# A mixture's first choice of experts is made in the attention layer in front of it

## The chip, the cores and the metric

The kernel runs as one program on one core of one Trainium2 chip. Its time is the device time of that core in microseconds, from one execution to the next; a profile of one execution shows every instruction on TensorE (PE, with its weight loads as PEld), VectorE (DVE), ScalarE (ACT), GpSimd (POOL) and the DMA queues (SyncE's among them, SP).

## What is computed

Eight layers are applied to x of 4 sequences, 1024 positions and 128 features, each as `x = x + layer(layernorm(x))`: a causal attention of 16 heads (AttentionA), a mixture of 8 experts, a gated attention, the same mixture again, a state space layer, a gated feed-forward layer, a second causal attention and the feed-forward layer again. The change bears on the two mixtures and the two layers in front of them. The mixture, cut to what matters:

```python
capacity = int(T / E * CAP_FACTOR)
probs = jax.nn.softmax(x @ Wr, axis=-1)
topk_probs, topk_experts = jax.lax.top_k(probs, K)
e_flat = topk_experts.reshape(B, S)
onehot = jax.nn.one_hot(e_flat, E, dtype=jnp.int32)
pos_all = jnp.cumsum(onehot, axis=1) - onehot
pos = jnp.take_along_axis(pos_all, e_flat[..., None], axis=-1)[..., 0]
keep = pos < capacity
buf = buf.at[e_flat, b_idx, pos_c].add(x_rep * keep[..., None])
h = jax.nn.relu(jnp.einsum('ebnc,ech->ebnh', buf, W1) + b1[:, None, None, :])
y = jnp.einsum('ebnh,ehc->ebnc', h, W2) + b2[:, None, None, :]
out = (y[e_flat, b_idx, pos_c] * keep * p_flat).reshape(B, T, K, C).sum(axis=2)
```

Every position picks its two likeliest experts (K = 2 of E = 8); each expert has 160 places per sequence, given out in the order of the positions, and what finds no place is dropped.

## The kernel before

x of all sequences stays in SBUF as eight chunks of 128 positions by 128 features per sequence (`k.xb(b)`). The layers follow one another in the list LAYERS; a layer opens its pools of SBUF and PSUM tiles when it begins and closes them at its end, and the pools of the next layer lie at the same addresses. Some layers (Begun) begin inside the layer in front of them: a Start object calls their first steps, with PSUM banks (`start.bank`) and an order (`start.pin`) lent by that layer. GatedAttention is begun inside the first mixture so. The mixture itself isn't: it begins when its layer is called.

A framework orders the instructions of each engine ahead of time, by their dependencies and their place in the program, and puts the semaphores in; an engine then works through its queue in order. Where the program wants an order of its own, it pins it: `k.order()` gives a function that chains instructions one behind the other on their engine. In all layers around the change the instructions on PE are pinned in the order of the program.

The mixture, Mixture.__call__, works through four sequences. For each, `normalized(b)` makes the normalised x, xl (L117 to L131: bn_stats, bn_aggr, Sqrt on ACT, reciprocal, eight TENSOR_SCALAR). `route(b)` is the choice, a generator that gives way at several points: eight transposes of xl into xt (L600, copied out of PSUM by DVE or ACT in turn, L108 and L110), the logits lg (L605), softmax over 8 experts (L617 to L624), the two best with ties broken by a rank table (L629 to L640), `taken` (L646); then the count of those before a position, cnt (L654), run and pos (L661, L662), spot (L665, L666), and rows and share for the later gather (L671 to L679). `dispatch(b)` builds for each chunk a 0/1 matrix d by comparing spot with the iota `place` (L691) and multiplies xl with it into the PSUM tiles acc (L696), which are copied to buf (L704). `experts(b)` runs the two matrices of every expert and calls the next sequence's route between them. So the choices of sequences 1 to 3 lie inside the experts of the sequence before, while that of sequence 0 stands at the head of the layer, before anything else of it:

```python
normalized(0)
for _ in route(0):
    pass
```

AttentionA works on 32 pairs of heads (n, eight per sequence), four groups gq of query blocks each. Small jobs wait in the list `pieces` and are called by `outputs(n, gq)`: one at the head of each of its steps (GROUPS gives 1, 1, 2 and 2 steps to the four groups), and a second one in a step when more than three wait. In a step the transposes of the probabilities p (L482) come first on PE, then the products of the step before with v (L497, into o), then scores further ahead (L374). Jobs are the projections, the product with Wo of a finished pair (L340, added to sum_t on DVE, L344), and after a sequence's last pair the transposes of sum_t (L350) and the addition to x (L352). All jobs share one PSUM bank, tag m, with a single buffer.

GatedAttention's `attend(b, other, before)` runs 16 steps for a sequence: a score product (L1012), bias on DVE (L1015), Relu and Square on ACT (L1018, L1019), and the product with v (L997) of the score of two steps before. In each step it also calls one step of `before` (output of the sequence before: L1037, L1042) and one of `other` (preparation of the next sequence). For the last sequence `other` is empty. Its bank for such steps, tag pt, has two buffers. After the steps the result is multiplied with ut (L1006) and then by the output weights (L1037).

Of the kernel before, what the change touches and what calls it, by code (L numbers as in the profile page):

```python
# [20 lines left out]
P = 128  # L21
B = 4
T = 1024
C = 128
NC = T // P
# [4 lines left out]
NEXP = 8  # L30
TOPK = 2
FF = 512
CAP = int(T / NEXP * 1.25)
# [143 lines left out]
class Start:  # L177

    def __init__(self, k, layer):
        self.k, self.open = k, True
        self.gen = layer.run(self)
        next(self.gen)

# [16 lines left out]
class AttentionA:  # L202
# [34 lines left out]
        )  # L237
        self.bo = k.broadcast_row(w, "bo", C, nc.sync)

    def __call__(self, start=None):  # L240
        k, tc, nc = self.k, self.k.tc, self.k.nc
        wq, wk, wv, wo, bo = self.wq, self.wk, self.wv, self.wo, self.bo
        Q, NQ, NP = self.Q, self.NQ, HEADS // 2
        scale = 1.0 / math.sqrt(DH_A)
        with self.stack as ctx:
# [14 lines left out]
            pieces = []  # L260
# [248 lines left out]
            for n in range(B * NP):  # L509
                for gq in range(NQ):  # L510
                    if gq == 1 and n + 3 < B * NP and (n + 3) % NP == 0:
                        normal = normalized((n + 3) // NP)
                    if 0 < gq < 3:
                        next(normal, None)
                    if gq == 0 and n + 2 < B * NP and (n + 2) % NP == 0:
                        across((n + 2) // NP)
                    if gq == 1 and n > 0:
                        joined(n - 1)
                    if gq == 3 and n + 2 < B * NP:
                        projected(n + 2)  # L520
                    outputs(n, gq)
            behind.pop(0)()
            joined(B * NP - 1)
            while pieces:
                pieces.pop(0)[1]()

# [4 lines left out]
class Mixture:  # L531
# [7 lines left out]
    def __init__(self, k: Kernel):  # L539
# [22 lines left out]
        self.ones = w.tile([P, P], F32, name="ones")  # L562
        nc.gpsimd.memset(self.ones, 1.0)

    def __call__(self, start=None):
        k, tc, nc, ex = self.k, self.k.tc, self.k.nc, self
        rows, share = self.rows, self.share
# [3 lines left out]
        with ExitStack() as ctx:  # L571
# [16 lines left out]
            def normalized(b):  # L588
                xls[b] = sb.tile([P, NC, C], F32, tag="xl", name="xl")
                k.normalize(xls[b], k.xb(b))  # L590

            def route(b):


                xl = xls[b]
                xt = sb.tile([P, T], F32, tag="xt", name="xt")
                for h in range(2):
                    ps = ps_t.tile([P, 512], F32, tag="pt", name="ps")
                    for c in range(4):
                        pe(nc.tensor.transpose(ps[:, c * P : (c + 1) * P], xl[:, h * 4 + c, :], k.ident))  # L600
                    k.evacuate(xt[:, h * 512 : (h + 1) * 512], ps)
                    yield
                lg = ps_l.tile([P, NC, NEXP], F32, tag="lg", name="lg")
                for c in range(NC):
                    pe(nc.tensor.matmul(  # L605
                        lg[:, c, :], xt[:, c * P : (c + 1) * P], ex.wr, start=True, stop=True
                    ))
                shape = [P, NC, NEXP]

                def wide(t):  # L610
                    return t.unsqueeze(2).to_broadcast(shape)

                def column(tag):
                    return k.small.tile([P, NC], F32, tag=tag, name=tag)

                top = column("top8")
                nc.vector.tensor_reduce(top, lg, AX.X, ALU.max)  # L617
                pr = sb.tile(shape, F32, tag="pr", name="pr")
                nc.vector.tensor_tensor(pr, lg, wide(top), ALU.subtract)
                nc.scalar.activation(pr, pr, AF.Exp)  # L620
                total = column("total")
                nc.vector.tensor_reduce(total, pr, AX.X, ALU.add)
                nc.vector.reciprocal(total, total)
                nc.vector.tensor_tensor(pr, pr, wide(total), ALU.mult)  # L624

                hot, prob, first = [], [], []
                for n in range(TOPK):
                    best = column(f"best{n}")
                    nc.vector.tensor_reduce(best, pr, AX.X, ALU.max)  # L629
                    h = sb.tile(shape, F32, tag=f"hot{n}", name="hot")  # L630
                    nc.vector.tensor_tensor(h, pr, wide(best), ALU.is_equal)

                    nc.vector.tensor_tensor(h, h, ex.rank.unsqueeze(1).to_broadcast(shape), ALU.mult)
                    r = column(f"rank{n}")
                    nc.vector.tensor_reduce(r, h, AX.X, ALU.max)
                    nc.vector.tensor_tensor(
                        h, wide(r), ex.rank.unsqueeze(1).to_broadcast(shape), ALU.is_equal
                    )
                    if n + 1 < TOPK:
                        nc.vector.scalar_tensor_tensor(pr, h, -2.0, pr, ALU.mult, ALU.add)  # L640
                    hot.append(h)
                    prob.append(best)
                    first.append(r)

                taken = sb.tile(shape, F32, tag="taken", name="taken")
                nc.vector.tensor_tensor(taken, hot[0], hot[1], ALU.add)  # L646
                yield
                yield
                yield

                cnt = ps_l.tile([P, 2, NC, NEXP], F32, tag="lg", name="cnt")
                flat = taken.rearrange("p c e -> p (c e)")
                for n, table in enumerate((ex.before, ex.ones)):
                    pe(nc.tensor.matmul(  # L654
                        cnt[:, n, :, :].rearrange("p c e -> p (c e)"), table, flat, start=True, stop=True
                    ))
                pos = sb.tile(shape, F32, tag="pos", name="pos")
                run = sb.tile(shape, F32, tag="run", name="run")
                nc.vector.memset(run[:, 0, :], 0.0)
                for c in range(1, NC):  # L660
                    nc.vector.tensor_tensor(run[:, c, :], cnt[:, 1, c - 1, :], run[:, c - 1, :], ALU.add)  # L661
                nc.vector.tensor_tensor(pos, cnt[:, 0, :, :], run, ALU.add)  # L662

                spot = sb.tile(shape, F32, tag="spot", name="spot")
                nc.vector.scalar_tensor_tensor(spot, pos, 1.0, taken, ALU.add, ALU.mult)  # L665
                nc.vector.tensor_scalar(spot, spot, -1.0, None, ALU.add)  # L666
                spots[b] = spot

                for n in range(TOPK):
                    mine = sb.tile(shape, F32, tag="mine", name="mine")  # L670
                    nc.vector.tensor_tensor(mine, hot[n], pos, ALU.mult)  # L671
                    at = column(f"at{n}")
                    nc.vector.tensor_reduce(at, mine, AX.X, ALU.add)
                    kept = column(f"kept{n}")
                    nc.vector.tensor_scalar(kept, at, float(CAP), None, ALU.is_lt)
                    nc.vector.tensor_tensor(share[:, b, :, n], kept, prob[n], ALU.mult)

                    nc.vector.tensor_scalar(at, at, float(CAP - 1), float(SLOTS), ALU.min, ALU.add)
                    nc.vector.scalar_tensor_tensor(  # L679
                        rows[:, b, :, n], first[n], -float(CAP), at, ALU.mult, ALU.add  # L680
                    )

            def dispatch(b, between):

# [114 lines left out]
                    if i + GOT < len(pairs):  # L799
                        fetch(i + GOT)  # L800

            normalized(0)
            for _ in route(0):
                pass
            left, behind = [], iter(())

            def close():
# [27 lines left out]
class GatedAttention(Begun):  # L835
# [37 lines left out]
    def run(self, start):  # L873
# [6 lines left out]
        with ExitStack() as ctx:  # L880
# [878 lines left out]
@with_exitstack  # L1759
def kernel(ctx: ExitStack, tc: tile.TileContext, ins: dict, out: bass.AP):  # L1760
    k = Kernel(ctx, tc, ins, out)
    made = {layer: layer(k) for layer in LOADS if layer in LAYERS}
    begun = None
    for n, layer in enumerate(LAYERS):
        layer = made[layer]
        if isinstance(layer, Begun):
            if begun is None:
                begun = Start(k, layer)
            begun.finish()
            begun = None  # L1770
# [113 lines left out]
```

## Time and profile before

| | us |
|---|---|
| three timed runs | 3298.49, 3306.97, 3306.78 |
| their median | 3306.78 |
| the profiled execution | 3300.56 |
| its span, first to last instruction | 3298.8 |
| AttentionA's last o product ends | 1152.74 |
| first mixture's first choice, from xl to spot | 1159.38 to 1174.94 |
| GatedAttention's last sequence, steps | 1557 to 1597 |
| second mixture's first choice, from xl to spot | 1602.78 to 1619.38 |
| instructions in all | 46096 |

The times in the lower rows are counted from the start of the span of the profiled execution. Busy times are sums over all layers, and the limits differ from layer to layer, so the part of the trace around a layer's border says more about this change than the totals. In lines of the order of time, the first number is the start, the second the length, then come engine, line, operation, the tile written, the tiles read and the shapes; "x8" stands for eight instructions drawn together, and the bracket gives the idle time before them with what ended it. Fp32 products appear twice per call.

### The profile page before, as it was taken

Reading aid. Unit: us, or ns where it says so; the run is one execution under the profiler, and the core shown is the slowest. Engines: PE = TensorE matmul, PEld = TensorE weight load, DVE = VectorE, ACT = ScalarE, POOL = GpSimd, SP = SyncE. Lnnn points to the kernel's source line nnn. Section 1 sums busy time; section 2 is a strip of 40 time slices with the busy share of each in tenths; the row PEclk is TensorE's granted clock in tenths of the full one; section 3 lists DMA queues with packets and bytes.
Section 4 is the critical chain, followed back from the end, with each engine's and each line's share of the span. In section 5 each row is a group of like instructions: output and inputs, shape, how many; then the busy total and the mean of one; then the engine's idle time right before and its main releaser. Section 6 shows DMA issues by size and latency. Waiting matters only on the chain. (4 is left out here: it accounts for less than half of the span.)

```text
span 3298.8 us, 46096 instructions
## 1 busy us (share of the span) xinstructions
PE 2965.1 (90%) x16624; PEld 1696.0 (51%) x16624; DVE 2324.5 (70%) x5415; ACT 1819.5 (55%) x3822; POOL 285.0 (9%) x297
## 2 busy tenths in 40 slices
PE   7999999999999988699898588888778899999988
PEld 4555555555555556445566244454445444444435
DVE  5777777778777666676564788888977767676634
ACT  4555555556555523355333797988643365556662
POOL 3000000000000013510034000000002101010000
PEclk9999999999999989899999799999998799899999
DMA  3110000000000001100011111111102111111100
GB/s 109 44 33 17 14 18 17 14 18 17 14 17 17 16 13 35 61 0 0 0 35 42 59 57 53 56 55 54 66 22 62 30 37 50 31 50 31 31 2 26
DMA packets 84901, 109.39 MB, mean 33 GB/s; under 512 B 26048, under 2 KB 66544, under 8 KB 82240
## 3 DMA queue, kind: packets, MB, share of 16 engines
q1 hardware_dynamic: 59136, 69.50, 6.6%
q0 software_dynamic: 18688, 30.65, 3.5%
q10 hardware_dynamic: 6848, 6.29, 0.6%
q8 instruction: 130, 2.13, 0.3%
q14 instruction: 99, 0.81, 0.1%
HBM read 90.76 MB, written 15.60 MB: 32 GB/s over the span
## 5 line engine op out<-in xcount | busy, mean ns | idle before, releaser
L389 ACT ACTIVATE p<-p,tops 128x640 f32<-128x640 f32 (+7 forms) x512 | 392.2, 768 | 287.6 <-DVE tops L387 226.3
L380 DVE CUSTOM_DVE_ANT_0 p<-s,mask 128x512 f32<-128x512 f32 (+3 forms) x768 | 392.1, 551 | 130.3 <-PE s L374 129.8
L1635 ACT ACTIVATE p<-x 128x512 f32<-128x512 f32 (+3 forms) x768 | 337.6, 490 | 246.3 <-PE x L1634 176.5
L1574 DVE TENSOR_REDUCE tops<-s 128x2 f32<-128x1024 f32 (+3 forms) x384 | 361.2, 955 | 133.5 <-PE s L1570 94.0
L1277 PE MATMUL acc<-hc,ident 128*128 128x512 f32 x512 | 269.7, 650 | 93.2 <-ACT hc L1276 92.4
L374 PE MATMUL s<-kt,qt 64*128 64x512 f32 (+3 forms) x1536 | 311.3, 516 | 20.2 <-DVE tops L380 19.8
L482 PEld LDWEIGHTS t<-ident,p 128*128 128x128 f32 x2304 | 263.0, 141 | 80.8 <-issue 66.7
L1264 DVE TENSOR_TENSOR_SCAN st<-decay,st 128x1024 f32<-128x1024 f32 x128 | 288.7, 2278 | 10.8 <-ACT decay L1261 10.3
L497 PE MATMUL o<-pt,vv 128*64 128x256 f32 (+1 forms) x2560 | 291.2, 365 | 0.0
L482 PE MATMUL t<-ident,p 128*128 128x128 f32 x2304 | 283.7, 273 | 1.6 <-ACT p L389 1.6
L1629 PE MATMUL x<-q,k 75*128 75x512 bf16 (+3 forms) x768 | 222.6, 337 | 27.8 <-ACT p L1635 15.0
L488 ACT COPY pt<-t 128x512 f32<-128x512 f32 (+1 forms) x320 | 155.0, 495 | 156.9 <-DVE pt L490 148.8
L1565 PE MATMUL s<-k,q 72*128 72x512 bf16 (+3 forms) x768 | 217.7, 350 | 24.4 <-DVE tops L1574 17.1
L1276 ACT ACTIVATE hc<-ps,by_time 128x256 f32<-128x256 f32 x512 | 200.3, 477 | 49.6 <-PE ps L1270 49.5
L490 DVE COPY pt<-t 128x512 f32<-128x512 f32 x320 | 212.2, 684 | 16.5 <-PE t L482 16.3
L497 PEld LDWEIGHTS o<-pt,vv 128*64 128x64 f32 x2560 | 166.8, 136 | 96.7 <-issue 28.6
L374 PEld LDWEIGHTS s<-kt,qt 64*128 64x128 f32 x1536 | 124.5, 187 | 146.0 <-issue 77.9
L1277 PEld LDWEIGHTS acc<-hc,ident 128*128 128x128 f32 x512 | 91.6, 198 | 208.9 <-ACT hc L1276 190.5
L1263 DVE TENSOR_TENSOR st<-du,bs 128x1024 f32<-128x1024 f32 x128 | 151.8, 1216 | 48.5 <-PE ps L1270 48.3
L696 PE MATMUL acc<-d,xl 128*128 128x480 f32 (+1 forms) x384 | 154.2, 563 | 28.0 <-DVE d L691 28.0
L1270 PEld LDWEIGHTS ps<-ident,st 128*128 128x128 f32 x1024 | 126.2, 147 | 96.3 <-issue 60.5
L1663 PE MATMUL o<-p,vx 128*32 128x512 f32 (+3 forms) x1536 | 171.8, 519 | 0.0
(302 smaller groups left out, 4763.8 us busy)
## 6 DMA issues: line engine op xcount, KB each, us to landing
bs<-b_rows SPq DMA_DIRECT2D x64, 512.0 KB
share<-shares SPq DMA_DIRECT2D x256, 64.0 KB
k<-b_parts POOLq DMA_DIRECT2D x16, 576.0 KB, 12.5
q<-b_parts POOLq DMA_DIRECT2D x48, 192.0 KB, 11.6
shares<-rows SPq DMA_DIRECT2D x512, 0.5 KB
b_parts<-part SPq DMA_DIRECT2D x24, 256.0 KB
w_W<-in_W_dram ACTq DMA_DIRECT2D x16, 256.0 KB
y_rows<-y SPq DMA_DIRECT2D x16, 192.0 KB
```

The source lines that it names most:

```text
L374: pe(nc.tensor.matmul(s[:, h, : hi - lo], q[feats, ib * P : (ib + 1) * P], kk[feats, lo:hi], start=True, stop=True,))
L380: ve(nc.vector.tensor_tensor_reduce(p[:, h, i, lo:hi], s[:, h, : hi - lo], m, -1.0, 3.4e38, ALU.add, ALU.min, tops[:, h, i, at : at + 1],))
L389: exp = nc.scalar.activation(p[:, h, i, :width], p[:, h, i, :width], AF.Exp, bias=tops[:, h, i, 0:1], scale=-1.0, accum_out=sums[:, h, i : ...
L482: pe(nc.tensor.transpose(t[:, m, h, i * P : (i + 1) * P], p[:, h, i, jb * P : (jb + 1) * P], k.ident))
L490: nc.vector.tensor_copy(pt[:, :, lo:], t[:, m, :, lo:])
L497: pe(nc.tensor.matmul(o[feats, lo:], pairs[n]["v"][:, jb, feats], pt[:, h, lo:], start=jb == 0, stop=jb == (gq + 1) * Q - 1,))
L1264: nc.vector.tensor_tensor_scan(st, decay, st, 0.0, ALU.mult, ALU.add)
L1277: nc.tensor.matmul(acc[:, c : c + 2, :].rearrange("p c d -> p (c d)"), k.ident, hc.rearrange("p c d -> p (c d)"), start=n == 0, stop=n == ...
L1565: start.pin(nc.tensor.matmul(s[:, a, : hi - lo], qq[:ROWS, two + a, ib * P : (ib + 1) * P], kk[:ROWS, two + a, lo:hi], start=True, stop=ha ...
L1574: nc.vector.tensor_reduce(tops[:, half, two : two + 2, n], s[:, :, : hi - lo], AX.X, ALU.max)
L1629: start.pin(nc.tensor.matmul(x[:, lo:], kk[:FULL, a, jb * P : (jb + 1) * P], qq[:FULL, a, hq * 512 + lo : (hq + 1) * 512], start=True, sto ...
L1635: nc.scalar.activation(p[:, a, lo:], x[:, lo:], AF.Exp)
```

## The change

The choice of sequence 0 becomes a method, `choice`, with the tiles and banks handed to it as arguments, and a second method, `early`, calls it from the layer in front of the mixture. The new tiles first (nine small matrices), mean and root are part of the constants, so that what is made early outlives the layer. Nothing of the computation differs. The body of `choice` is that of `route` word for word, but for the tiles: lg and cnt are now parts of a whole bank, and pr, hot, taken and the others come from `make`.

```diff
+        self.first = w.tile([P, 9, NC, NEXP], F32, name="first")
+        self.mean = w.tile([P, NC, nc.vector.BN_AGGR_DIM], F32, name="mean")
+        self.root = w.tile([P, NC], F32, name="root")
+
+    def early(self, x, xl, xt, bank, pin):
+        nc = self.k.nc
+        self.spot = None
+        stats = self.k.small.tile([P, NC, nc.vector.BN_STATS_DIM], F32, tag="stats", name="stats")
+        for c in range(NC):
+            nc.vector.bn_stats(stats[:, c, :], x[:, c, :])
+        for c in range(NC):
+            nc.vector.bn_aggr(self.mean[:, c, :], stats[:, c, :])
+        nc.scalar.activation(self.root, self.mean[:, :, 1], AF.Sqrt, bias=self.k.eps)
+        yield
+        nc.vector.reciprocal(self.root, self.root)
+        self.scaled(xl, x)
+        yield
+        tiles = iter(range(9))
+
+        def make(tag):
+            return self.first[:, next(tiles)]
+
+        yield from self.choice(0, xl, xt, bank, bank, pin, make)
+
+    def scaled(self, xl, x):
+        for c in range(NC):
+            self.k.nc.vector.tensor_scalar(
+                xl[:, c, :], x[:, c, :], self.mean[:, c, 0:1], self.root[:, c : c + 1], ALU.subtract, ALU.mult
+            )
```

`choice` gives way after each half of xt, three times after `taken`, and ends with spot, rows and share. In AttentionA the steps become pieces of the last pair of heads, and what is left is run before the last pair's product with Wo:

```diff
+                    if gq == 1 and n + 1 == B * NP:
+                        begun = mixture.early(
+                            k.xb(0), one.tile([P, NC, C], F32, tag="xl", name="xl"),
+                            one.tile([P, T], F32, tag="xt", name="xt"),
+                            lambda: ps_m.tile([P, 512], F32, tag="m", name="ps"), pe,
+                        )
+                        pieces.extend([(None, lambda: next(begun, None))] * 7)
                     outputs(n, gq)
             behind.pop(0)()
             joined(B * NP - 1)
+            for _ in begun:
+                pass
             while pieces:
                 pieces.pop(0)[1]()
```

In GatedAttention they take the place of the empty `other` of the last sequence:

```diff
-                before = attend(b, prepare(b + 1) if b + 1 < B else iter(()), before)
+                if b + 1 < B:
+                    other = prepare(b + 1)
+                else:
+                    other = start.mixture.early(
+                        k.xb(0), ln_sb.tile([P, NC, C], F32, tag="xl", name="xl"),
+                        ln_sb.tile([P, T], F32, tag="xt", name="xt"), start.bank, start.pin,
+                    )
+                before = attend(b, other, before)
```

The mixture then begins with the scaling alone, which writes xl of sequence 0 once more, into its own tile:

```diff
-            normalized(0)
-            for _ in route(0):
-                pass
+            xls[0] = sb.tile([P, NC, C], F32, tag="xl", name="xl")
+            ex.scaled(xls[0], k.xb(0))
+            spots[0] = ex.spot
```

The rest passes the mixture on to the layer in front of it:

```diff
-        after = made[LAYERS[n + 1]] if n + 1 < len(LAYERS) else None
-        begun = Start(k, after) if isinstance(after, Begun) else None
-        layer(begun)
+        after, second = ([made[a] for a in LAYERS[n + 1 : n + 3]] + [None, None])[:2]
+        begun = Start(k, after, second) if isinstance(after, Begun) else None
+        layer(begun, after) if isinstance(after, Mixture) else layer(begun)
```

More of the change, by code (lines that the diff above doesn't have):

```diff
@@ L177, with __init__ @@
 class Start:
-    def __init__(self, k, layer):
-        self.k, self.open = k, True
+    def __init__(self, k, layer, mixture=None):
+        self.k, self.open, self.mixture = k, True, mixture
         self.gen = layer.run(self)
@@ L238, in __init__, with __call__ @@
         self.bo = k.broadcast_row(w, "bo", C, nc.sync)
-    def __call__(self, start=None):
+    def __call__(self, start=None, mixture=None):
         k, tc, nc = self.k, self.k.tc, self.k.nc
@@ new lines, in scaled, with choice, wide, column @@
+    def scaled(self, xl, x):
[3 more added lines that the diff above has]
+            )
+    def choice(self, b, xl, xt, bank, bank_l, pe, make):
+        k, nc, ex, rows, share = self.k, self.k.nc, self, self.rows, self.share
+        SLOTS = NEXP * CAP
+        for h in range(2):
+            ps = bank()
+            for c in range(4):
+                pe(nc.tensor.transpose(ps[:, c * P : (c + 1) * P], xl[:, h * 4 + c, :], k.ident))
+            k.evacuate(xt[:, h * 512 : (h + 1) * 512], ps)
+            yield
+        lg = bank_l()[:, : NC * NEXP].rearrange("p (c e) -> p c e", c=NC)
+        for c in range(NC):
+            pe(nc.tensor.matmul(
+                lg[:, c, :], xt[:, c * P : (c + 1) * P], ex.wr, start=True, stop=True
+            ))
+        shape = [P, NC, NEXP]
+        def wide(t):
+            return t.unsqueeze(2).to_broadcast(shape)
+        def column(tag):
+            return k.small.tile([P, NC], F32, tag=tag, name=tag)
+        top = column("top8")
+        nc.vector.tensor_reduce(top, lg, AX.X, ALU.max)
+        pr = make("pr")
+        nc.vector.tensor_tensor(pr, lg, wide(top), ALU.subtract)
+        nc.scalar.activation(pr, pr, AF.Exp)
+        total = column("total")
+        nc.vector.tensor_reduce(total, pr, AX.X, ALU.add)
+        nc.vector.reciprocal(total, total)
+        nc.vector.tensor_tensor(pr, pr, wide(total), ALU.mult)
+        hot, prob, first = [], [], []
+        for n in range(TOPK):
+            best = column(f"best{n}")
+            nc.vector.tensor_reduce(best, pr, AX.X, ALU.max)
+            h = make(f"hot{n}")
+            nc.vector.tensor_tensor(h, pr, wide(best), ALU.is_equal)
+            nc.vector.tensor_tensor(h, h, ex.rank.unsqueeze(1).to_broadcast(shape), ALU.mult)
+            r = column(f"rank{n}")
+            nc.vector.tensor_reduce(r, h, AX.X, ALU.max)
+            nc.vector.tensor_tensor(
+                h, wide(r), ex.rank.unsqueeze(1).to_broadcast(shape), ALU.is_equal
+            )
+            if n + 1 < TOPK:
+                nc.vector.scalar_tensor_tensor(pr, h, -2.0, pr, ALU.mult, ALU.add)
+            hot.append(h)
+            prob.append(best)
+            first.append(r)
+        taken = make("taken")
+        nc.vector.tensor_tensor(taken, hot[0], hot[1], ALU.add)
+        yield
+        yield
+        yield
+        cnt = bank_l()[:, : 2 * NC * NEXP].rearrange("p (n c e) -> p n c e", n=2, c=NC)
+        flat = taken.rearrange("p c e -> p (c e)")
+        for n, table in enumerate((ex.before, ex.ones)):
+            pe(nc.tensor.matmul(
+                cnt[:, n, :, :].rearrange("p c e -> p (c e)"), table, flat, start=True, stop=True
+            ))
+        pos = make("pos")
+        run = make("run")
+        nc.vector.memset(run[:, 0, :], 0.0)
+        for c in range(1, NC):
+            nc.vector.tensor_tensor(run[:, c, :], cnt[:, 1, c - 1, :], run[:, c - 1, :], ALU.add)
+        nc.vector.tensor_tensor(pos, cnt[:, 0, :, :], run, ALU.add)
+        spot = make("spot")
+        nc.vector.scalar_tensor_tensor(spot, pos, 1.0, taken, ALU.add, ALU.mult)
+        nc.vector.tensor_scalar(spot, spot, -1.0, None, ALU.add)
+        self.spot = spot
+        for n in range(TOPK):
+            mine = make("mine")
+            nc.vector.tensor_tensor(mine, hot[n], pos, ALU.mult)
+            at = column(f"at{n}")
+            nc.vector.tensor_reduce(at, mine, AX.X, ALU.add)
+            kept = column(f"kept{n}")
+            nc.vector.tensor_scalar(kept, at, float(CAP), None, ALU.is_lt)
+            nc.vector.tensor_tensor(share[:, b, :, n], kept, prob[n], ALU.mult)
+            nc.vector.tensor_scalar(at, at, float(CAP - 1), float(SLOTS), ALU.min, ALU.add)
+            nc.vector.scalar_tensor_tensor(
+                rows[:, b, :, n], first[n], -float(CAP), at, ALU.mult, ALU.add
+            )
@@ L592, in route @@
             def route(b):
-                xl = xls[b]
                 xt = sb.tile([P, T], F32, tag="xt", name="xt")
[L597 to L681, printed above, removed]
+                yield from ex.choice(
+                    b, xls[b], xt, lambda: ps_t.tile([P, 512], F32, tag="pt", name="ps"),
+                    lambda: ps_l.tile([P, 512], F32, tag="lg", name="lg"), pe,
+                    lambda tag: sb.tile([P, NC, NEXP], F32, tag=tag, name=tag),
+                )
@@ L683, in dispatch @@
+                spots[b] = ex.spot
             def dispatch(b, between):
@@ L1048, in run @@
             for b in range(B):
-                before = attend(b, prepare(b + 1) if b + 1 < B else iter(()), before)
+                if b + 1 < B:
[4 more added lines that the diff above has]
+                        ln_sb.tile([P, T], F32, tag="xt", name="xt"), start.bank, start.pin,
+                    )
+                before = attend(b, other, before)
             for _ in before:
```

## The prediction

> **What bounds the kernel now.** I read the page's busy shares first, then the stretches around the two places where an attention layer ends and a mixture begins, then the order of time on PE and on DVE there. TensorE leads the whole:
>
> ```profile
> PE 2965.1 (90%) x16624; PEld 1696.0 (51%) x16624; DVE 2324.5 (70%) x5415; ACT 1819.5 (55%) x3822; POOL 285.0 (9%) x297
> ```
>
> The table of stretches (length, busy time of PE, PEld, DVE, ACT, POOL, granted clock, DMA share, GB/s) shows the last pair of heads of AttentionA (1113 to 1153), its end with the first choice of experts, and for GatedAttention the last sequence (1557 to 1597) and the first choice of the second mixture:
>
> ```profile
> 1113.00:1153.00 40.00, 37.82 (x285) 24.37 (x284) 26.16 (x84) 21.27 (x50) 0.00 (x0) 1.00 0.06 18
> 1153.00:1177.00 24.00, 9.96 (x41) 7.16 (x40) 16.76 (x78) 2.43 (x4) 0.26 (x1) 0.64 0.00 1
> ...
> 1557.00:1597.00 40.00, 40.00 (x118) 19.73 (x117) 16.31 (x39) 20.36 (x32) 0.00 (x0) 1.00 0.00 0
> ```
>
> Both attention layers end with PE full and DVE at 65% and 41%; then comes a stretch in which PE works 42% of the time at a mean clock of 0.64. PE in order of time says why (start, length, line, what it waited for):
>
> ```profile
> 1158.08 0.66 PE L350 MATMUL ps<-ident,sum_t 128*128 128x128 f32 x4 [0.85 <-DVE x L352]
> 1159.92 1.09 PE L600 MATMUL ps<-ident,xl 128*128 128x128 f32 x4 [1.19 <-issue]
> 1162.16 1.12 PE L600 MATMUL ps<-ident,xl 128*128 128x128 f32 x4 [1.15 <-DVE xt L108]
> 1163.07 3.42 PE L605 MATMUL lg<-w_Wr,xt 128*128 128x8 f32 x16
> 1171.70 0.66 PE L654 MATMUL cnt<-taken,before 128*128 128x64 f32 x2 [5.21 <-DVE rstd L129]
> 1172.16 0.64 PE L654 MATMUL cnt<-taken,ones 128*128 128x64 f32 x2
> 1176.86 18.66 PE L696 MATMUL acc<-d,xl 128*128 128x480 f32 x46 [4.07 <-DVE d L691]
> ```
>
> From the end of AttentionA's last transposes (1158.74) to the first dispatch product (1176.86) 18.1 us pass; PE does some 7 us of the choice in them, at half clock for the most part. The rest is a serial chain on DVE. The second place has the same picture:
>
> ```profile
> 1601.78 3.73 PE L1037 MATMUL ps<-w_owT,gated 128*128 128x128 f32 x32
> ...
> 1608.39 2.02 PE L605 MATMUL lg<-w_Wr,xt 128*128 128x8 f32 x16
> 1616.14 0.66 PE L654 MATMUL cnt<-taken,before 128*128 128x64 f32 x2 [5.74 <-DVE taken L646]
> ...
> 1621.30 18.85 PE L696 MATMUL acc<-d,xl 128*128 128x480 f32 x48 [4.07 <-DVE d L691]
> ```
>
> There DVE's last product with ut (L1006) ends at 1602.67, so 18.6 us lie between it and the first dispatch product. Two more rows, on DVE at the first place, are needed for the sum: the scaling of x and the end of the count.
>
> ```profile
> 1159.38 2.13 DVE L131 TENSOR_SCALAR xl<-x,mv,rstd 128x128 f32<-128x128 f32 x8
> ...
> 1172.83 1.36 DVE L661 TENSOR_TENSOR run<-cnt,run 128x8 f32<-128x8 f32 x7 [1.16 <-PE cnt L654]
> 1174.23 0.22 DVE L662 TENSOR_TENSOR pos<-cnt,run 128x64 f32<-128x64 f32 x1
> 1174.49 0.22 DVE L665 SCALAR_TENSOR_TENSOR spot<-pos,taken 128x64 f32<-128x64 f32 x1
> ```
>
> **What stays at each place.** The mixture still has to write xl of sequence 0 (8 TENSOR_SCALAR, 2.13 us), now a second time. Its tiles lie where the layer in front had its own: xl began at 1159.38, after the last transposes of sum_t, although nothing in it needs them, and at the second place at 1602.78, 0.1 us after the last use of ut, with DVE idle for 3.5 us before. I read that as the pool being free only then, and keep it: nothing of the mixture but `place` starts before. Next in program order is xl of sequence 1 (8 more, 2.13 us; its statistics lie earlier, since of the 64 bn_stats of L123 before 1180 only 8 start after 1050), then d (1.49 us), on which the dispatch waits. First place: one x<-ps,x of 0.69 us, 16 x 0.266 = 4.26, d 1.49, 0.1 for the hand-over: 6.5 us instead of 18.1. Second: two x<-ps,x at a pitch of 0.6, 4.26, 1.49, 0.1: 7.0 instead of 18.6. Taken away: 11.6 and 11.6 us.
>
> The slow start of the dispatch stays, too: the first six products ran from 1176.86 to 1181.0, where the later sets take 2.15 us. Another dispatch, at 1755.96, came after only 4.39 us of idle PE and had 12 products in 6.89 us, at 0.57 each against 0.36. A gap of 6.5 us will do the same, so I take nothing; should the clock hold, 2.0 us more are won at each place.
>
> **What AttentionA pays.** The choice issues 28 PE instructions per place (8 transposes, 16 for lg, 4 for cnt), about 47 on DVE beside the statistics, 2 or 3 on ACT, and no DMA; SP and POOL get nothing. With the pieces taken one or two per step, the statistics and the scaling fall in the step of 1135, the transposes at 1139 and before 1142, lg ahead of the transposes of p at 1142.1, the count after the last o product (1152.74).
> - Transposes at full clock: two sets at a pitch of 0.43 (the set at 1639.99 took 0.60 with its tail): 0.9 us. lg at 1645.73 took 1.85. Sum 2.7 on a full PE.
> - lg must wait for the second xt copy, since both use the one bank of tag m. That copy is ACT's (L110, 0.58 us), and ACT has the two Exp of 1142.02 and 1143.16 (2.3 us) there. But PE idles 1.57 us at that place for the same Exp. Lower bound: lg fills that idle time, and 1 us is left of the 2.7; upper: the copy comes after both Exp and everything lies bare, 4 us. I take 2.6.
> - The count: cnt takes the bank of tag m in PE's order ahead of the two last Wo products (L340), which can't start before pos has read it: 1171.70 to 1174.45, 2.75 us, nearly all bare. Queued behind on PE are L340, then the sum_t transposes, then the dispatch. At half clock in the before; at full clock 0.3 less, with the last o product's `ot` (0.42) ahead of it on DVE. I take 2.75.
> - DVE's top-2 chain (1166.5 to 1171.55, 5 us) lies in 1147 to 1153, where DVE has 2.6 us of work in 7. The later ops on rows and share fill DVE's waits between L344 and L352. Zero; without that cover they cost up to 2 us.
>
> Shift of AttentionA's end 5.4 us (3.5 to 9). Net 11.6 - 5.4 = 6.2 us won (2.5 to 8).
>
> **What GatedAttention pays.** PE has no gap in 1557 to 1597 and the choice falls into the first 8 of 16 steps. PE: 0.9 + 1.85 + 0.85 (cnt at 1693.72 to 1694.28 and 1743.52 to 1744.18 took 0.56 to 0.66; at most the 1.1 of above) = 3.6 us bare. Two banks, so no wait for pos. DVE is idle 1.88 us in each step of 2.57, ACT 1.28; a score tile r is used two steps after it is made, so a delay of r by up to some 5 us lies beside PE's own work. taken must be there three steps (7.7 us) after lg; its chain took 5.1 and 5.6 us. Bound: it comes late by up to 2.5 us with r in between. I take 0. Net 11.6 - 3.6 = 8.0 us (5 to 8).
>
> [...] The table load before the Sqrt at 1565.46 took 1.28 us and the Sqrt began 1.30 us after it; the following Relu and Square needed no other load. So one Exp load and the Exp (1.28 + 0.26) cost ACT 1.5 us, in idle time of 1.28 per step: nothing for PE. [...]
>
> **Sum.** 6.2 + 8.0 = 14.2 us. The profiled execution took 3300.56 us (span 3298.8), so it would take 3286.4. It lies 6.2 us under the median of the three timed runs, 3306.78, and 2 above their lowest, 3298.49; the mean of all four is 3303.2, and 3303.2 - 14.2 = **3289 us** is the forecast.
>
> **Rivals.**
> - *Larger gain.* d of the first chunk is put ahead of xl of sequence 1: only its own xl is needed. For it: in other waits DVE's order was filled with whatever was ready. Against: at 1602.78 to 1608.8 all 16 scalings came in one row. It saves 2.13 at each place: gain 18.5, 3303.2 - 18.5 = 3285 us. Chance 0.2.
> - *Half a gain.* The same mechanism with the upper bounds of the prices: lg bare behind the two Exp (+1.4), the late rows and share ops in front of sum_t (+2), taken late in GatedAttention (+2.5): gain 14.2 - 5.9 = 8.3, 3295 us. For it: PE's order is written out by hand, so one late piece holds all behind it. Chance 0.2.
> - *Slower: the chain is not hidden in front.* Each PE instruction of the choice waits for the DVE or ACT step before it, and PE stands with it. From xl to pos the choice lasted 15.1 us (1159.38 to 1174.45) in the open. Laid bare in both attention layers it costs 15.1 each against 11.6 won: +7, 3310 us. It decides once PE waits over 11.6 us per layer. For it: one bank in AttentionA. Against: DVE has 14 us free of 40 there and 24 in GatedAttention, with 2.5 to 5 us between pieces. Chance 0.1.
>
> **How the numbers follow.** Main case 0.5, with a range of its own from the bounds: gains of 7.5 to 16. The others 0.2, 0.2, 0.1. What can be told from no change is about 0.3%, 9.9 us. The main case lies beyond it with 0.9, the larger gain wholly, half a gain with 0.15: faster 0.45 + 0.2 + 0.03 = 0.68. The slower case exceeds it only in part, but a stall in a layer whose PE order is fixed can be larger than its open length: 0.1. Same 0.22. Range: from a gain of 18.5 plus 2 x 2.0 for the clock (3281) with 2 us for the run-to-run spread, to no gain at all (3303): 3279 to 3303.
>
> **What would show it.** L340 of the last pair of heads 5.4 us later against the last o product's old place, with a wait of about 1.8 us for DVE pos before it; 6.5 and 7 us from the last L350, and from the last L1006, to the first dispatch product; 16 scalings ahead of d; the step time in GatedAttention 2.57 us but for added PE work. I am wrong if the mixture's xl or d waits for something other than its pool, or if PE in the two tails shows new waits of over 10 us together.

## The result and the profile after

The changed kernel takes 3291.48 us (3286.93 to 3294.25) against 3306.78 (3298.49 to 3310.57): a ratio of 0.9955, with a 95% interval of 0.9942 to 0.9969. That is 15.3 us less, 10 to 19 by the interval; the forecast was 3289. The two profiled executions lie closer together, 3300.56 and 3294.25, because the one of before lies near the low end of its kernel's times and the one of after at the high end. So the places of the change are read from the traces, and the total from the timed runs.

The busy shares have hardly moved:

```profile
PE 2965.0 (90%) x16624; PEld 1695.2 (51%) x16624; DVE 2329.3 (71%) x5431; ACT 1820.4 (55%) x3822; POOL 284.9 (9%) x297
```

No work is gone (the 16 more DVE instructions are the two repeated scalings); it has moved. PE in order of time at the first place, from AttentionA's last scores to the first dispatch product:

```profile
1139.12 1.13 PE L374 MATMUL s<-kt,qt 64*128 64x512 f32 x4
...
1142.29 1.08 PE L497 MATMUL o<-pt,vv 128*64 128x256 f32 x8
1143.31 0.66 PE L614 MATMUL ps<-ident,xl 128*128 128x128 f32 x4
1145.96 3.19 PE L619 MATMUL ps<-w_Wr,xt 128*128 128x8 f32 x16 [2.00 <-ACT xt L110]
1149.01 3.65 PE L482 MATMUL t<-ident,p 128*128 128x128 f32 x16
1152.59 2.04 PE L497 MATMUL o<-pt,vv 128*64 128x256 f32 x16
...
1159.90 0.39 PE L668 MATMUL ps<-first,ones 128*128 128x64 f32 x2
1162.10 1.10 PE L340 MATMUL ps<-ot,w_Wo 128*128 128x512 f32 x2 [1.81 <-DVE first L676]
1164.07 2.07 PE L340 MATMUL ps<-ot,w_Wo 128*128 128x512 f32 x2 [0.88 <-DVE sum_t L344]
...
1168.89 1.12 PE L350 MATMUL ps<-ident,sum_t 128*128 128x128 f32 x4 [0.85 <-DVE x L352]
1176.34 19.52 PE L749 MATMUL acc<-d,xl 128*128 128x480 f32 x48 [6.33 <-issue]
```

The chain that stood in the open, transposes, lg and count (L614, L619, L668), now lies inside AttentionA's tail, with two waits: 2.00 us before lg, which needs the second xt copy from ACT, and 1.81 us before the last pair's products with Wo (L340), which need the one bank back from the count. After the last transposes 6.33 us pass to the dispatch, 18.1 before. But the lines also run slow: lg takes 3.19 and the 16 transposes of p 3.65, where the same work takes 1.85 at the second place (below) and 1.75 for 14 transposes later in this tail. The table of stretches tells why (stretch, its length, busy time and instructions of PE, PEld, DVE, ACT and POOL, granted clock, DMA share, GB/s):

```profile
1142.90:1146.40 3.50, 1.50 (x14) 0.88 (x10) 0.96 (x3) 3.01 (x7) 0.00 (x0) 1.00 0.00 0
1146.40:1149.80 3.40, 3.40 (x18) 3.40 (x18) 0.45 (x2) 0.09 (x1) 0.00 (x0) 0.50 0.07 23
1149.80:1153.20 3.40, 3.40 (x18) 2.88 (x18) 1.74 (x5) 0.75 (x2) 0.00 (x0) 0.50 0.05 18
1153.20:1156.60 3.40, 3.40 (x34) 2.61 (x32) 2.90 (x12) 0.71 (x2) 0.00 (x0) 0.99 0.00 0
```

After the stretch with the wait the granted clock is 0.50 for 6.8 us, in which PE does 36 instructions; the next 3.4 us alone hold 34. What the last scores set off until the dispatch begins has come down only from 38.0 to 36.7 us, counted from the last of the four score products. Before, they stood here:

```profile
1138.36 1.13 PE L374 MATMUL s<-kt,qt 64*128 64x512 f32 x4
```

The second place, PE and then DVE:

```profile
1570.12 1.85 PE L619 MATMUL ps<-w_Wr,xt 128*128 128x8 f32 x16
...
1604.11 3.73 PE L1090 MATMUL ps<-w_owT,gated 128*128 128x128 f32 x32
1612.00 20.13 PE L749 MATMUL acc<-d,xl 128*128 128x480 f32 x48 [4.15 <-issue]
```

```profile
1604.32 0.69 DVE L1059 TENSOR_TENSOR gated<-acc,ut 128x512 f32<-128x512 f32 x1 [0.17 <-PE acc L1050]
1605.12 1.37 DVE L602 TENSOR_SCALAR xl<-x,mean,root 128x128 f32<-128x128 f32 x5
```

Here lg waits for nothing (no bracket) and runs at full clock. The mixture's first own instruction, the scaling, comes 0.1 us after the last use of ut, as before. From the first score product of the last sequence to the dispatch it is 55.8 us, where it was 64.3; that product, before and after:

```profile
1557.01 1.02 PE L1012 MATMUL ps<-q 128*128 128x512 f32 x2
1556.23 1.02 PE L1065 MATMUL ps<-q 128*128 128x512 f32 x2
```

Nearly all the traced gain so comes from the second place: 8.5 us there, 1.3 at the first. Some of it is lost again just behind: the 48 products of the second dispatch take 20.13 us, 18.85 before, because 5.5 us of them run at half clock instead of 2.8. By their end the second place has won 7.2 us, and the first 1.0.

### The profile page after: what moved, and what is told of

Same layout as the page of the kernel before. It is cut to its first block, busy times and chain, and to the rows that moved or that the text cites. A ratio compares the mean times of both kernels' runs of the same rounds, so it can differ in the third digit from the quotient of the medians.

```text
span 3292.5 us, 46106 instructions
## 1 busy us (share of the span) xinstructions
PE 2965.0 (90%) x16624; PEld 1695.2 (51%) x16624; DVE 2329.3 (71%) x5431; ACT 1820.4 (55%) x3822; POOL 284.9 (9%) x297
## 5 line engine op out<-in xcount | busy, mean ns | idle before, releaser
L1324 DVE TENSOR_TENSOR_SCAN st<-decay,st 128x1024 f32<-128x1024 f32 x128 | 288.8, 2279 | 11.0 <-ACT decay L1321 10.5
L490 DVE COPY pt<-t 128x512 f32<-128x512 f32 x320 | 212.2, 684 | 17.1 <-PE t L482 17.0
## 6 DMA issues: line engine op xcount, KB each, us to landing
q<-b_parts POOLq DMA_DIRECT2D x48, 192.0 KB, 11.8
```

Source lines behind the costliest of these rows:

```text
L1324: nc.vector.tensor_tensor_scan(st, decay, st, 0.0, ALU.mult, ALU.add)
```

## The experiments

The runs share one table. "Tail A" goes from the start of AttentionA's last score product to the start of the first dispatch product; "tail G" from the first score product of GatedAttention's last sequence to the second mixture's first dispatch product; both are from each kernel's trace. The last two columns are the time of the timed runs and its ratio to before with the 95% interval.

| kernel | tail A, us | tail G, us | median, us | ratio |
|---|---|---|---|---|
| before | 38.0 | 64.3 | | |
| after | 36.7 | 55.8 | 3291.48 | 0.9955 (0.9942 to 0.9969) |
| e1, choice early in GatedAttention only | 39.6 | 55.8 | 3296.67 | 0.9973 (0.9960 to 0.9986) |
| e2, choice early in AttentionA only | 36.7 | 65.9 | 3304.09 | 1.000 (0.999 to 1.001) |
| e3, tiles only | 39.6 | 64.3 | 3302.22 | 0.9991 (0.9980 to 1.0002) |
| e4, the changed kernel again | 36.7 | 55.8 | 3287.18 | 0.9942 (0.9927 to 0.9958) |
| e5, xt copies on DVE | 33.8 | 55.8 | 3290.37 | 0.9957 (0.9941 to 0.9973) |
| e6, lg and count in another bank | 29.0 | 55.8 | 3286.83 | 0.9939 (0.9921 to 0.9957) |
| e7, both | 28.7 | 55.8 | 3283.72 | 0.9937 (0.9916 to 0.9958) |
| e8, both, and the first d ahead of the next xl | 26.2 | 53.1 | 3278.00 | 0.9912 (0.9893 to 0.9932) |

e1 to e4 share one set of runs of before (median 3304.41), e5 to e8 another (3304.19). Line numbers in the kernels of e5 to e8 are one to three above those of after.

### e1, e2, e3 and e4: which part brings the time

e1 takes the early choice out of AttentionA, e2 out of GatedAttention, e3 out of both; a mixture whose choice was not made early makes it at its head, as before. The tiles that outlive the layers, and the two methods, stay in all of them. e4 is the changed kernel unaltered.

```diff
-                    if gq == 1 and n + 1 == B * NP:
-                        begun = mixture.early(
...
-                        pieces.extend([(None, lambda: next(begun, None))] * 7)
...
-            for _ in begun:
-                pass
...
-            xls[0] = sb.tile([P, NC, C], F32, tag="xl", name="xl")
-            ex.scaled(xls[0], k.xb(0))
-            spots[0] = ex.spot
+            if ex.spot is not None:
+                xls[0] = sb.tile([P, NC, C], F32, tag="xl", name="xl")
+                ex.scaled(xls[0], k.xb(0))
+                spots[0] = ex.spot
+            else:
+                normalized(0)
+                for _ in route(0):
+                    pass
```

That is e1; e2 has the second half of it and this, and e3 has all:

```diff
-                if b + 1 < B:
-                    other = prepare(b + 1)
-                else:
-                    other = start.mixture.early(
...
-                before = attend(b, other, before)
+                before = attend(b, prepare(b + 1) if b + 1 < B else iter(()), before)
```

Expected of e1:

> Only GatedAttention makes the choice early; the first mixture makes its own in the open, as in the kernel before. Theory 1 (the trace pair): the whole gain is made here. In GatedAttention the first dispatch product came 8.5 us earlier, against 1.1 us in AttentionA: this kernel is 8.5 us faster than the kernel before, ratio 0.9974, and within 2 us of the changed one. Theory 2 (the parts win alike, and the profiled execution of the changed kernel was a slow one): half of 15 us, ratio 0.9977; not told apart by this run alone, but by the next.

of e2:

> Only AttentionA makes the choice early; the second mixture makes its own in the open. Theory 1: AttentionA's tail loses 10.7 us where the mixture's head wins 11.8, so 1 us faster than before, ratio 0.9997. Theory 2: 7 us faster, ratio 0.998. In the profile theory 1 wants lg to wait about 2 us for the second xt copy on ACT, and the products after it at half clock.

of e3:

> Neither layer makes the choice early; only the three new constant tiles (2.4 KB per partition) and the method calls remain. If 5 us of the gain came from moved addresses or another order in the rest of the program, and not from the choice, this kernel is 5 us faster than before (0.9985). By theories 1 and 2 it is the kernel before: ratio 1.000, no new gap anywhere.

and of e4:

> The changed kernel once more, beside the same runs of the kernel before as the three others. Theory 1: 9.6 us by the trace pair, ratio 0.9971. Theory 2: about 15 us, ratio 0.9955 again.

Measured: e1 wins 8.9 us (0.27% of 3304; 5 to 13), e2 nothing (3 either way), e3 3.0 (from 7 won to 1 lost), e4 19 (14 to 24). The traces agree with the first two: tail G is 8.5 us shorter wherever GatedAttention makes the choice, and tail A 1.3 us shorter than before's where AttentionA makes it. So of the two parts only the early choice in GatedAttention wins by itself, and the one in AttentionA, by e2 and the traces, is worth next to nothing as it stands. In e2's trace the untouched second place took 65.9 us, 1.6 more than before, which takes its 1.3 back. The tiles cost nothing that can be seen. The 0.9971 that the pair of traces would give lies outside e4's interval: the whole change wins more than that pair shows.

Two things don't close. The first: the parts add up to 9 us where the whole brings 15 to 19. The intervals of the parts are 4 and 3 us wide to each side and that of the whole about 5, but e1's (5 to 13) and e4's (14 to 24) don't touch: taken out of the whole, AttentionA's part costs 9.5 us by the medians, and alone, in e2, it brings nothing. The granted clocks of the timed runs show where a part of the rest lies. The clock records of the traces of before and after hold only 1.00 and 0.50 (some 309 and 306 us of the latter), so a mean clock of 0.9522 (the 29 runs of before) stands for about 316 us at half clock; e1 has 306, e2 318 and e4 297. In the pair of traces the half clock that begins at the two places fell by only 3.4 us (34.1 us before, 30.7 after). So most of it would lie in stages that the change doesn't touch; why it does is not shown.

The second: in e1 and e3, whose tail A holds no early work, it took 39.6 us instead of before's 38.0: their traces show 3.4 us at half clock from 1144.9 and 1144.1, which before's trace doesn't have. By that comparison the early choice in AttentionA wins 2.9 us instead of 1.3. I give it as 1.3 to 2.9.

### e5, e6 and e7: why AttentionA gives so little

Two causes were to be told apart: the engine of the second xt copy (ACT, which stands behind two Exp of 1.15 and 1.13 us), and the single bank of tag m, which lg and the count share with xt and with the products with Wo. ACT in order of time in the changed kernel shows the first:

```profile
1142.31 1.15 ACT L389 ACTIVATE p<-p,tops 128x1024 f32<-128x1024 f32 x1 [2.72 <-DVE tops L387]
...
1143.46 1.13 ACT L389 ACTIVATE p<-p,tops 128x1024 f32<-128x1024 f32 x1
...
1144.59 0.83 ACT L488 COPY pt<-t 128x512 f32<-128x512 f32 x2
1145.32 0.59 ACT L110 COPY xt<-ps 128x512 f32<-128x512 f32 x1
```

The transposes for that copy were done at about 1144; it began at 1145.32 and lg at 1145.96.

e5 puts both xt copies of the early choice in AttentionA on DVE; e6 takes lg and the count out of tag m into the score tiles' banks; e7 does both.

```diff
                             lambda: ps_m.tile([P, 512], F32, tag="m", name="ps"), pe,
+                            copy=nc.vector.tensor_copy,
...
-            k.evacuate(xt[:, h * 512 : (h + 1) * 512], ps)
+            (copy or k.evacuate)(xt[:, h * 512 : (h + 1) * 512], ps)
```

```diff
                             lambda: ps_m.tile([P, 512], F32, tag="m", name="ps"), pe,
+                            bank_l=lambda: ps_s.tile([P, 2, 512], F32, tag="s", name="s")[:, 0, :],
...
-        yield from self.choice(0, xl, xt, bank, bank, pin, make)
+        yield from self.choice(0, xl, xt, bank, bank_l or bank, pin, make)
```

Expected of e5:

> The changed kernel, but in AttentionA both xt copies of the early choice are DVE's; one of them was ACT's and stood behind two Exp. Theory 1: PE's 2.0 us wait before lg falls to some 0.8 us, the clock stays at 1.00, lg takes 1.85 instead of 3.19 and the next 16 transposes 1.85 instead of 3.65: the first dispatch product of the first mixture comes 4 to 5 us earlier against AttentionA's last scores, and the kernel is 4 us faster than the changed one (ratio to before 0.9943). Rival: DVE is the busy engine there and its pt copies come late instead: no gain. Second rival: the clock falls anyway, since the tail after it is thin: only 1.2 us.

of e6:

> The changed kernel, but in AttentionA lg and cnt lie in a buffer of the three of tag s, not in the one bank of tag m. Theory 1: the 1.81 us wait of L340 for pos goes, and lg of the first half needn't wait for the second xt copy, so lg starts 2 us earlier, but its second half still waits for the copy: 2 to 3 us faster than the changed kernel. Rival: the transposes of p need that buffer and wait instead: no gain or a loss of 1 to 2 us.

and of e7:

> Both of the two before: copies on DVE and lg and cnt in a buffer of tag s. Theory 1: no wait of PE over 0.5 us in AttentionA's last pair but that for p, the clock at 1.00 up to the last Wo product, AttentionA's tail 4 us longer than in the kernel before instead of 10.7: 6 to 7 us faster than the changed kernel, ratio to before about 0.9935. Rivals as above.

e5, PE in order of time:

```profile
1141.93 1.95 PE L620 MATMUL ps<-w_Wr,xt 128*128 128x8 f32 x16 [0.78 <-DVE xt L616]
1143.74 3.56 PE L482 MATMUL t<-ident,p 128*128 128x128 f32 x16
...
1156.43 1.10 PE L340 MATMUL ps<-ot,w_Wo 128*128 128x512 f32 x2 [1.81 <-DVE first L677]
```

The wait before lg falls from 2.00 to 0.78 us and lg runs in 1.95, but the 16 transposes behind it still take 3.56: the clock goes to half at 1143.9 for 3.4 us. The wait of 1.81 at the count stays, as it should. Tail A is 33.8 us, 2.9 better than in after, where 4 to 5 had been expected with the clock whole. In time e5 can't be told from after.

e6, PE in order of time:

```profile
1145.26 0.96 PE L620 MATMUL s<-w_Wr,xt 128*128 128x8 f32 x8
1147.42 1.06 PE L620 MATMUL s<-w_Wr,xt 128*128 128x8 f32 x8 [1.21 <-ACT xt L110]
1148.33 1.94 PE L482 MATMUL t<-ident,p 128*128 128x128 f32 x16
...
1157.21 0.39 PE L669 MATMUL s<-first,ones 128*128 128x64 f32 x2
1157.43 1.08 PE L340 MATMUL ps<-ot,w_Wo 128*128 128x512 f32 x2
...
1163.09 0.66 PE L350 MATMUL ps<-ident,sum_t 128*128 128x128 f32 x4 [0.85 <-DVE x L352]
```

The first eight products of lg, which need only the first half of xt, now run while the second is being copied; the rest waits 1.21 us for the same ACT copy. L340 follows the count with no wait. And the clock stays whole up to 1164.0, so the 16 transposes take 1.94. Tail A is 29.0 us, 7.7 better than in after, where 2 to 3 had been expected. It adds up: from the second xt transposes to the end of the 16 transposes 9.3 us in after and 5.5 here (3.8); the next 16 o products 2.04 and 1.73 (0.3); the wait for pos (1.8); from the first L340 to the end of the last L350 7.9 and 6.3 (1.6): 7.5. Only 2.6 us of this are shorter waits (2.00 to 1.21, and the 1.81); the rest is the same products at full clock instead of half.

e7, PE in order of time:

```profile
1143.08 2.00 PE L621 MATMUL s<-w_Wr,xt 128*128 128x8 f32 x16
1144.94 1.95 PE L482 MATMUL t<-ident,p 128*128 128x128 f32 x16
...
1160.16 1.11 PE L350 MATMUL ps<-ident,sum_t 128*128 128x128 f32 x4 [0.85 <-DVE x L352]
```

No wait is left before lg, and tail A comes to 28.7 us, 0.3 better than e6: the wait of 1.21 us is gone, but here half clock from 1158.2 catches both L350, which takes 0.9 back. So the shared bank was the larger cause by the traces, and the copy's engine is worth about 1 us more once the bank is its own. The timed runs of e6 and e7 have intervals that overlap with after's; that they are better rests on the traces' tails, one trace each. These can be compared to within some 1.6 us, by which the unaltered tail of e1 and e3 differs from before's; with the change, after, e2 and e4 all have 36.7.

### e8: the first d ahead of the next sequence's xl

One rival of the forecast was a larger gain, with d built ahead of the second scaling. In the changed kernel 16 scalings stand ahead of d at both places, the order in the program: `normalized(b + 1)` stands in front of `dispatch(b)`. e8 is e7 with the second scaling handed to the dispatch as what it does later.

```diff
-                if b + 1 < B:
+                if b > 0 and b + 1 < B:
                     normalized(b + 1)
-                buf = dispatch(b, close)
+                buf = dispatch(b, close if b else lambda: normalized(1))
```

> As the one before, and the scaling of sequence 1 comes after the first two chunks of d in program order. Theory 1: 2.1 us less between the end of the front layer and the first dispatch product in each mixture (4.2 us in place of 6.3, 4.9 in place of 7.0), which is the larger gain of the prediction: 4 us faster than the kernel before this one, ratio to before about 0.992. Rival: the order on DVE doesn't change, or the start of the dispatch is bound by something else: nothing.

DVE in order of time at the first place, in after and then in e8:

```profile
1170.66 2.13 DVE L602 TENSOR_SCALAR xl<-x,mean,root 128x128 f32<-128x128 f32 x8
1172.71 2.13 DVE L131 TENSOR_SCALAR xl<-x,mv,rstd 128x128 f32<-128x128 f32 x8
1174.76 4.29 DVE L744 TENSOR_TENSOR d<-place,first 128x1280 f32<-128x1280 f32 x3
```

```profile
1161.38 2.13 DVE L604 TENSOR_SCALAR xl<-x,mean,root 128x128 f32<-128x128 f32 x8
1163.43 2.88 DVE L746 TENSOR_TENSOR d<-place,first 128x1280 f32<-128x1280 f32 x2
1166.24 2.13 DVE L131 TENSOR_SCALAR xl<-x,mv,rstd 128x128 f32<-128x128 f32 x8
```

PE in e8, first place and second:

```profile
1165.02 19.79 PE L751 MATMUL acc<-d,xl 128*128 128x480 f32 x48 [4.28 <-issue]
...
1598.63 4.54 PE L751 MATMUL acc<-d,xl 128*128 128x480 f32 x12 [1.50 <-issue]
1604.04 13.16 PE L751 MATMUL acc<-d,xl 128*128 128x480 f32 x36 [0.87 <-DVE d L746]
```

PE's gap before the dispatch is 4.28 us instead of 6.33 at the first place and 1.50 instead of 4.15 at the second; the tails are 2.5 and 2.7 us shorter than in e7. After the 1.50 the clock holds: e8's trace has no half clock at the second place (its 48 products take 0.38 and 0.37 us each), where before had 13.7 us of it and after 6.8. e8 takes 3278.00 us, at 0.9912 (0.9893 to 0.9932) of before: 29 us less, 22 to 35, where the two tails are 11.8 and 11.2 shorter than before's, 23 together. Its interval lies under the one first measured for the change (0.9942 to 0.9969) and meets that of e4 only at its edge, so it is the version to keep. Its interval overlaps with e7's (0.9916 to 0.9958): what the order on DVE brings is read from the two tails.

## Why the prediction was right, and where it was wrong

**What stays at each place** was predicted at 6.5 and 7.0 us and measured at 6.33 (from the end of L350, 1170.01, to 1176.34) and 6.99 (from 1605.01 to 1612.00). The reading behind it held: the mixture's own xl starts when the layer in front ends, and 16 scalings come ahead of d.

**GatedAttention's price** was predicted at 3.6 us and measured at 3.1: the time from the last sequence's first score product to the end of L1059 went from 45.66 to 48.78. The gain there was predicted at 8.0 and measured at 8.5. The table loads, of which both traces hold 103 in all, cost what the prediction had them at: one took 1.28 us, ACT's Sqrt began 1.30 us after its load (1564.68, 1565.98), and the load for Exp ran while ACT waited for DVE:

```profile
1570.64 1.28 ACT L634 ACT_TABLE_LOAD   x1
1572.52 0.26 ACT L634 ACTIVATE first<-first 128x64 f32<-128x64 f32 x1 [0.60 <-DVE first L633]
```

**AttentionA's price** is the step that failed: 5.4 us were predicted, with 9 as the upper end, and 10.5 were measured (from the start of the last four score products to the end of the last L350, 20.4 before and 30.9 after), or 8.9 against the 22.0 of e1 and e3. L340, forecast 5.4 us later, came 8.6 later. Term by term, against before:

| term | predicted, us | measured, us |
|---|---|---|
| two sets of transposes | 0.9 | 1.0 |
| lg, net of the idle time that it fills | 1.7 | 4.9 |
| the count, and L340 waiting for pos | 2.75 | 2.5 |
| the o products behind lg | 0 | 0.3 |
| L340 and L350 | 0 | 1.9 |

Transposes and count were right, down to the wait of 1.81 us that the prediction put at about 1.8. Two terms were off. For transposes and lg together I took 2.6 us, about midway between the bounds of 1 and 4, and 5.9 were measured, above even the upper one. Its condition is what happened: the copy comes after both Exp, everything lies bare, and PE stood 2.00 us. And I let a stall cost its own length. The clock went to half behind it, which made lg 3.19 us instead of 1.95, the 16 transposes 3.65 instead of 1.95, and the o products 0.3 longer; the second half-clock stretch, from 1163.5, caught L340 and L350 (7.9 us instead of 6.0). For the dispatch I had asked what the clock would do, but not for the tail that I was stretching. The gain at this place was put at 6.2 us (2.5 to 8) and came to 1.3 to 2.9.

One reading was wrong at no cost: the statistics and the scaling of the early choice did not fall in the step of 1135. The framework placed them at 796 to 829 us, long before. The slow start of the dispatch, taken as unchanged, became 1.3 us longer at the second place.

**The sum** was 14.2 us; the two places give 9.8 by the pair of traces, or 11.4 with the larger figure for AttentionA. The timed runs give 15.3 (10 to 19), 19 (14 to 24) when repeated. So the forecast's time is met more closely than its parts deserve, and that is luck: the parts fell short by 3 to 4 us, and a gain that the forecast didn't hold came on top. Of the 4 to 9 us that remain, a part goes with the lower half-clock time of the timed runs, as said with e4; the cause stays open. In the stages behind the second dispatch the same code differs by some us between executions: the second causal attention, from its first score product to its last output product, took 666 to 675 us in these traces, with 96 to 115 us at half clock in it.

**The rivals.** The slower case did not come: PE's new waits in AttentionA are 2.00 and 1.81 us, under the 11.6 from which it would decide, and GatedAttention has none. The larger gain did not come by itself, but e8 shows its price was right: 2.1 us of PE's gap at the first place, when the program puts d first. Of the three conditions of half a gain, the first came true (lg bare behind both Exp, in AttentionA). The late rows and share steps cost little: in e6, at full clock, L340 and L350 take 6.3 us against before's 6.0. And taken came in time in GatedAttention, where PE shows no wait before the count.

## What to carry to other kernels

Here the step moved into a layer whose PE order is fixed needed a PSUM bank of its own before it needed a faster engine: the bank gave 7.7 us of the tail, the engine 2.9, and both together 8.0, in one trace each and more by the clock than by the waits themselves. Price a new stall in such an order at its length and at the half clock that may follow it (here 2.00 us, then 6.8 at half clock), and check the tail behind it as well as the stage it was moved from. Where one border sets everything free at once, the place in the program decides what comes first; put first what the bounding engine waits for (here d: PE's gap went from 6.33 us to 4.28 at the first place).

## What was not expected of the hardware

At the two places half clock lasted 20.5 and 13.7 us in before's trace, and 6.8, 17.1 and 6.8 us in after's. It came behind some short waits of PE and not behind others:

| kernel, place | PE's wait | then, at half clock |
|---|---|---|
| after, before lg | 2.00 us | 6.8 us |
| e5, before lg | 0.78 us | 3.4 us |
| e6, inside lg | 1.21 us | none |
| e7, before lg | none | none |
| after, second dispatch | 4.15 us | 6.8 us |
| e8, second dispatch | 1.50 us | none |

The wait alone doesn't order them: half clock came behind 0.78 us in one place and not behind 1.21 us in another. Nor does the code: in before and e1 the last scores start at 1138.36 and 1138.39, and the same products with the same two waits for p (0.88 and 0.69 us; 0.87 and 0.69) follow, but e1's trace has 3.4 us at half clock from 1144.9, and before's has none until 1159.9. What decides it is not shown: no run here varies the waits by themselves.
